# Channel attention over depthwise convolutions: edge products, transposes and mixing placed between the images of a gram, and one PSUM pool for convolution and gram

## The chip, the cores and the metric

The kernel runs on one core of a Trainium2 chip. The metric is device time in microseconds (us) of one execution, as the median of several runs. Besides, one execution was recorded by the hardware profiler; its profile and trace carry all other times here.

The engines: PE multiplies matrices (PEld is its weight load), DVE (VectorE), ACT (ScalarE) and POOL (GpSimd) work on vectors, SP issues most DMAs. PE writes PSUM alone, which has eight banks of 128 x 512 fp32 numbers. [...]

## What is computed

The input is a batch of B = 4 images with C = 192 channels of 128 x 128 pixels, fp32. Two layers follow each other. The change lies in the first, cut here to what matters:

```python
qkv = dwconv3x3(conv1x1(x, w_qkv), w_dw)      # 1x1, then a depthwise 3x3
q, k, v, l = jnp.split(qkv, 4, axis=1)
q, k, v = (heads(q), heads(k), heads(v))      # 8 heads of 24 channels: (b, 8, 24, h*w)
q = q / jnp.maximum(jnp.linalg.norm(q, axis=-1, keepdims=True), EPS)
k = k / jnp.maximum(jnp.linalg.norm(k, axis=-1, keepdims=True), EPS)
attn = jnp.einsum('bhcn,bhdn->bhcd', q, k) * temperature[None]
attn = jax.nn.softmax(attn, axis=-1)
out = jnp.einsum('bhcd,bhdn->bhcn', attn, v).reshape(b, c, h, w)
...                                            # a gate L from l
out = conv1x1(L + out + x, w_proj) + L
```

So for each head and image a 24 x 24 matrix over all 16384 pixels is needed, from q and k after their 3x3 convolution, and the norms of q's and k's channels. The second layer is a dilated local attention, and the change doesn't touch it.

## The kernel before, in words

Three stages run one after the other.

1. `project` (L382) multiplies x by the 1x1 weights, writes q and k before their 3x3 convolution to `qk_dram` in DRAM, and convolves v.
2. `channel_attention` (L671) convolves q and k, makes the attention matrices and multiplies them into the projection ("mixing", `mix1` and `mix2`), so that the second pass can apply both in one product. This is where the change lies.
3. `second_pass` (L962) applies them and does the second layer.

In stage 2, `head` (L919) is called for eight heads. A head has 48 channels to convolve: 24 of q, then 24 of k. The image's 128 rows lie on 128 partitions, in four strips of 32 rows. `loaded` (L700) fetches two channels of each of four groups for all four images, eight channels ("a source", six to a head, 2 MB each, seven DMAs on SP), into one of three buffers: two of `u` and one lent by the second pass (`lent`). It also fetches the 3x3 taps (`few`), and POOL spreads them into a band matrix (L731, L733). `convolve` (L736) multiplies one of the three columns of taps for one channel into a PSUM bank: four matmuls on four 32 x 32 parts of the array, each of which the chip runs as two weight loads and two matmuls. `order` (L925) interleaves the columns of neighbouring channels. `evicted` (L749) copies a finished bank to `conv` on ACT, and DVE takes its statistics.

A band matrix knows only its own strip. The two rows at each of the three edges between strips lack the neighbour's row there. They are made once more, by themselves, from four rows around the edge ("cut"):

- `cut_loaded` (L773) loads these rows of q and of k, 192 KB each, by two DMAs on SP. Each of the two buffers exists once, so a load waits until the product of the edge before is done with it.
- `cut_convolved` (L783) is the edge's product: six matmuls into a PSUM bank, and two copies to `s_cut` on ACT.
- `cut_turned` (L804) transposes it image by image on PE ("a turn"), and ACT copies it to `cut`.
- `cut_squares` (L812) adds its squares to the norms on DVE.

In `head` the loads for the three edges stand at channels n = 12, 28 and 44 of the order, the products after n = 14, 30 and 46, and the turns of the first two after n = 18 and 34.

`products` (L819) then makes the gram: for each of four images 32 matmuls of 128 x 96 columns accumulate in one bank (L824). After the first image stands the third turn. Then come `kept` (L831) and `part` (L837) on DVE, which pick and sum the wanted entries; the corner products of the cuts (L844, 12 matmuls); and the small sums (L854 to L862) that fold both into `logits` and give the norms. `finish` (L870) is a generator: `step` runs it one piece further after every fourth channel of the next head: norms, softmax, and in its last two pieces the mixing (L900) for two images each, its copy on DVE (L901) and its stores to `mix1` or `mix2` by DMAs on SP (L904, L907). Ahead of the heads' pieces, the same list holds those of two gates.

What sets the order: on PE the program's order is kept as written (`manual_schedule`). On the other engines and on SP's queue the framework orders instructions by the program's order among those that are ready in its own model, and sets all semaphores. PSUM is split into six banks for convolutions, edges and turns (`papc`), one for the gram and the mixing (`papg`) and one for the small sums and gates (`paps`).

Of the kernel before, what the change touches and what calls it, by code (L numbers as in the profile page):

```python
# [7 lines left out]
F32 = mybir.dt.float32  # L8
# [5 lines left out]
B, C, H, W = 4, 192, 128, 128  # L14
# [4 lines left out]
HALF = 96  # L19
# [651 lines left out]
def channel_attention(tc, d, load, qk_dram, mix1, mix2, band_p, u_p, gate_p, lent, gates):  # L671
# [7 lines left out]
    with ExitStack() as ctx:  # L679
# [4 lines left out]
        few_p = ctx.enter_context(tc.tile_pool(name="pax", bufs=2))  # L684
        st = ctx.enter_context(tc.tile_pool(name="pas", bufs=1))
        fin = ctx.enter_context(tc.tile_pool(name="paf", bufs=1))
        ps_c = ctx.enter_context(tc.tile_pool(name="papc", bufs=6, space=bass.MemoryType.PSUM))
        ps_g = ctx.enter_context(tc.tile_pool(name="papg", bufs=1, space=bass.MemoryType.PSUM))
        ps_s = ctx.enter_context(tc.tile_pool(name="paps", bufs=1, space=bass.MemoryType.PSUM))

        bands = [band_p.tile([128, 4, 2, 3, STRIP], F32, tag=f"band{k}", name=f"band{k}") for k in range(2)]
# [78 lines left out]
                both.append(t)  # L770
            return both

        def cut_loaded(hd, edge):  # L773
            us = []
            for which in range(2):
                c0 = which * C + hd * CH0
                u = cut_p.tile([4 * CH0, B * W], F32, tag=f"u{which}", name=f"cut{which}_{hd}_{edge}")
                first = (edge + 1) * STRIP - 2
                nc.sync.dma_start(u, qk_dram[first : first + 4, c0 : c0 + CH0].rearrange("r c b w -> r c (b w)"))
                us.append(u)  # L780
            return us

# [33 lines left out]
                for r in range(2):  # L816
                    nc.vector.tensor_add(sq, sq, square[:, :, which, r * CH0 : (r + 1) * CH0])

        def products(hd, q, sq, k, sk, cuts, s_cut):  # L819
            gram = ps_g.tile([HALF, B, HALF], F32, tag="gram", name=f"gram{hd}")  # L820
            for b in range(B):
                for v in range(W // 4):
                    four = lambda a: a[:, b, v].rearrange("p c w -> p (c w)")
                    nc.tensor.matmul(gram[:, b, :], four(q), four(k), start=v == 0, stop=v == W // 4 - 1)  # L824
# [12 lines left out]
            nc.vector.reduce_sum(part, kept.rearrange("p b c w -> p (b c) w"), axis=AX.X)  # L837

            two = 2 * CH0
            sums = ps_s.tile([128, SM], F32, tag="sm", name=f"sm{hd}")  # L840
            extra = sums[:two, EXTRA:].rearrange("p (b c) -> p b c", b=B)
            for b in range(B):
                for edge, cut in enumerate(cuts):
                    nc.tensor.matmul(  # L844
                        extra[:, b, :], cut[:, b, 0], cut[:, b, 1], start=edge == 0, stop=edge == 2
                    )
            own = st.tile([two, B, CH0], F32, tag="own", name=f"own{hd}")
            other = st.tile([two, B, CH0], F32, tag="other", name=f"other{hd}")
            for r, to in enumerate((own, other)):
                pick_row = same_row[:, r : r + 1].unsqueeze(1).to_broadcast([two, B, CH0])  # L850
                nc.vector.tensor_mul(to, extra[:, :, r * CH0 : (r + 1) * CH0], pick_row)
            nc.vector.tensor_add(own, own, other)
            sm = sums[:CH0]
            nc.tensor.matmul(sm[:, : B * CH0], fold, part, start=True, stop=False)  # L854
            nc.tensor.matmul(
                sm[:, : B * CH0], fold_rows, own.rearrange("p b c -> p (b c)"), start=False, stop=True
            )
            nc.tensor.matmul(
                sm[:, B * CH0 : 2 * B * CH0], ones[:, :CH0], sk.rearrange("p b c -> p (b c)"), start=True, stop=True
            )  # L860
            for b in range(B):
                nc.tensor.matmul(  # L862
                    sm[:, 2 * B * CH0 + b : 2 * B * CH0 + b + 1], sq[:, b, :], ones[:, :1], start=True, stop=True
                )
            by_image = lambda a: a.rearrange("p (b c) -> p b c", b=B)
            nc.vector.tensor_copy(logits[:, :, hd % 2, :], by_image(sm[:, : B * CH0]))
            nc.vector.tensor_copy(nk[:, :, hd % 2, :], by_image(sm[:, B * CH0 : 2 * B * CH0]))
            nc.vector.tensor_copy(nq[:, :, hd % 2], sm[:, 2 * B * CH0 : EXTRA])

        def finish(hd):  # L870


            rows, norm_q, norm_k = logits[:, :, hd % 2, :], nq[:, :, hd % 2], nk[:, :, hd % 2, :]
            wide = lambda a: a.unsqueeze(2).to_broadcast([CH0, B, CH0])
            for a in (norm_q, norm_k):
                nc.scalar.activation(a, a, AF.Sqrt)
            yield
# [12 lines left out]
            nc.vector.reciprocal(tot, tot)  # L890
            nc.vector.tensor_mul(rows, rows, wide(tot))
            yield
            yield
            low = min(max(128 - hd * CH0, 0), CH0)
            for b in range(0, B, 2):
                mixed = fin.tile([CH0, 2, C], F32, tag="mixed", name=f"mixed{hd}_{b}")
                pm = ps_g.tile([HALF, B, HALF], F32, tag="gram", name=f"pm{hd}_{b}")
                two = pm.rearrange("p b c -> p (b c)")[:CH0].rearrange("p (h o) -> p h o", h=2)
                for e in range(2):
                    nc.tensor.matmul(two[:, e, :], logits[:, b + e, hd % 2, :], wph[:, hd, :], start=True, stop=True)  # L900
                nc.vector.tensor_copy(mixed, two)  # L901
                for e in range(2):
                    if low:
                        nc.sync.dma_start(mix1[b + e][hd * CH0 : hd * CH0 + low], mixed[:low, e, :])  # L904
                    if low < CH0:
                        at = G + hd * CH0 + low - 128
                        nc.sync.dma_start(mix2[b + e][at : at + CH0 - low], mixed[low:, e, :])  # L907
                yield

        pending = [gate(ps_s) for gate in gates]  # L910

        def step():
            while pending:
# [5 lines left out]
        def head(hd):  # L919
# [6 lines left out]
            sources, pcs, sums, us, taps, s_cuts, cuts = {}, {}, [], [], [], [], []  # L926
# [22 lines left out]
            products(hd, fulls[0], sums[0], fulls[1], sums[1], cuts, s_cuts[2])  # L949
            pending.append(finish(hd))  # L950

        same, same_row, fold, fold_rows, ones, ident, wph, tempr = (
# [645 lines left out]
```

## Time and profile before

| | us |
|---|---|
| median of 3 runs | 4379.28 (4377.39 to 7416.38) |
| the profiled execution | 4374.27 |
| its span, first to last instruction | 4372.3 |
| stage 2 in the span | about 824 to 1592 |
| first convolution matmul after the small sums, heads 1 to 7 | 951.90, 1043.90, 1132.91, 1222.00, 1312.30, 1403.09, 1495.05 |
| first gram matmul, heads 0 to 7 | 926.75, 1018.74, 1107.75, 1196.84, 1287.15, 1377.93, 1469.89, 1556.11 |
| last gram matmul of the last head | 1578.3 |

The mean granted clock of PE is 0.978 of full speed. Of a line in the groups of instructions, the parts are: line, engine, operation, output and inputs, shapes, count; then busy time and mean of one in ns; then the idle time before them and what ended it. In the list of waits, "A <- B" is A's engine standing idle until B, with total us, times and the longest. "issue" is a wait whose cause the profile doesn't name. In the chain, each piece has its start and its length in us.

### The profile page before, as it was taken

The page shows a single profiled execution, that of the slowest core. Times are in us where ns is not written, and L with a number is a line of the kernel's source. Part 1 is how long each engine was busy: PE and PEld are TensorE (multiplying, and loading weights), DVE is VectorE, ACT ScalarE, POOL GpSimd, SP SyncE. Part 2 cuts the span into 40 slices and gives each one's busy share as a digit, 9 for nine tenths or more (in the row PEclk, how much of TensorE's full clock was granted, in tenths as well). Part 3 has the DMA queues.
Part 4 walks back from the last instruction along what each step waited for, and adds up shares of the span by engine and source line. Part 5 has one row for each costly group of instructions (what it writes and reads, how often), then busy time and mean ns, then how long its engine had stood idle before and what let it go on. Part 6 is the DMA issues. An engine that isn't in the chain of part 4 may idle for free.

```text
span 4372.3 us, 74543 instructions
## 1 busy us (share of the span) xinstructions
PE 4159.7 (95%) x25728; PEld 1669.8 (38%) x25728; DVE 3818.5 (87%) x5572; ACT 2632.4 (60%) x4906; POOL 3407.6 (78%) x3411
## 2 busy tenths in 40 slices
PE   8999999889899889899999999999999999999996
PEld 3333333355565543333333333333333333333331
DVE  6999999856556547899999999999999999999996
ACT  6999999734334447455665656656556566566531
POOL 6888888633323205899999999999999999999998
PEclk9999999899999999999999999999999999999997
DMA  7888888767766647656656666555555665555521
GB/s 234 265 270 251 271 274 267 217 150 171 169 156 156 165 114 157 118 124 131 131 129 133 124 133 134 126 125 130 128 130 124 137 134 124 131 130 129 116 52 32
DMA packets 476106, 676.89 MB, mean 155 GB/s; under 512 B 135937, under 2 KB 311501, under 8 KB 475729
## 3 DMA queue, kind: packets, MB, share of 16 engines
q1 hardware_dynamic: 437840, 505.39, 42.4%
q0 software_dynamic: 37888, 166.74, 20.6%
q8 instruction: 204, 3.34, 0.3%
q14 instruction: 174, 1.42, 0.1%
HBM read 278.18 MB, written 201.33 MB: 110 GB/s over the span
## 4 chain that ended last, share of the span: by engine, by line
PE 71%; DVE 14%; DMA 5%; issue 5%; POOL 3%; ACT 2%; SPq 1%; DVEq 0%; POOLq 0%; ACTq 0%
PE sc L1256 9%; PE ex L1378 8%; PE ph L1023 8%; PE pu L427 6%; PE pkv L1177 5%; PE pc L741 5%; DVE term L1384 4%; PE gram L824 4%; PE pkv L1180 4%; PE q L1237 4%; PE q L1234 4%; PE pu L432 3%; DVE prod L1245 3%; PE po L1400 2%; PE pu L578 2%
## 5 line engine op out<-in xcount | busy, mean ns | idle before, releaser
L1387 POOL TENSOR_TENSOR acc<-acc,term 128x512 f32<-128x512 f32 x1536 | 2037.6, 1332 | 144.6 <-DVE term L1384 58.2
L1384 DVE TENSOR_TENSOR term<-ex,vring 128x512 f32<-128x512 f32 (+2 forms) x1596 | 998.6, 662 | 57.3 <-PE ex L1378 44.4
L1245 DVE TENSOR_TENSOR prod<-q,kring 128x1536 f32<-128x1536 f32 (+1 forms) x600 | 1006.4, 1686 | 20.4 <-PE q L1234 10.8
L504 POOL TENSOR_TENSOR v_True<-v_True,side 128x512 f32<-128x512 f32 (+1 forms) x512 | 643.9, 1270 | 127.0 <-ACT side L493 97.9
L1378 PE MATMUL ex<-e_sb,spread 108*128 108x512 bf16 x1728 | 567.3, 387 | 49.9 <-DVE term L1384 32.5
L481 DVE SCALAR_TENSOR_TENSOR pa<-vboth,dwv,pa 128x1024 f32<-128x1024 f32 (+1 forms) x448 | 574.3, 1282 | 43.0 <-ACT pa L474 14.5
L1190 ACT COPY kring<-pkv 64x512 f32<-64x512 f32 x384 | 223.7, 583 | 415.6 <-PE pkv L1180 410.2
L1075 DVE SCALAR_TENSOR_TENSOR pa<-hboth,posw,pa 128x1024 f32<-128x1024 f32 (+1 forms) x320 | 408.1, 1275 | 37.5 <-ACT pa L1063 18.6
L1256 PE MATMUL sc<-prod,pick 128*32 128x512 f32 x3456 | 428.6, 598 | 1.8 <-DVE prod L1245 1.8
L752 DVE BATCH_NORM_STATS2 stats<-conv 128x6 f32<-128x128 f32 x1536 | 306.8, 279 | 114.9 <-ACT conv L750 112.2
L1378 PEld LDWEIGHTS <-spread 108*128 108x128 bf16 x1728 | 133.3, 97 | 661.3 <-issue 641.0
L1023 PE MATMUL ph<-lent,mix 128*64 128x512 f32 (+1 forms) x1024 | 375.5, 598 | 1.8 <-DMA mix<-mixed 1.8
L427 PE MATMUL pu<-xt,wx 128*128 128x512 f32 x768 | 360.6, 613 | 17.2 <-ACT vboth L463 10.2
L1403 ACT COPY o<-po 128x512 f32<-128x512 f32 x192 | 106.3, 588 | 446.2 <-PE po L1400 240.0
L1177 PE MATMUL pkv<-y,wkv 128*128 128x512 f32 x768 | 363.7, 595 | 9.5 <-DMA y<-moved 9.3
L493 ACT ACTIVATE side<-ring,dwv 128x512 f32<-128x512 f32 (+1 forms) x512 | 348.4, 725 | 31.8 <-POOL v_True L504 27.9
L733 POOL COPY band<-few 32x6 f32<-32x6 f32 x384 | 75.3, 199 | 372.0 <-PE pc L741 247.6
L1107 ACT ACTIVATE side<-hring,posw 128x512 f32<-128x512 f32 (+1 forms) x512 | 341.7, 713 | 11.7 <-DMA side<-side 9.8
L750 ACT COPY conv<-pc 128x512 f32<-128x512 f32 x384 | 216.8, 586 | 187.4 <-PE pc L741 178.4
L741 PE MATMUL pc<-u,band 32*32 32x508 f32 (+1 forms) x6144 | 281.3, 624 | 36.6 <-issue 22.1
L1190 ACT COPY vring<-pkv 64x512 f32<-64x512 f32 x384 | 224.3, 584 | 45.5 <-PE pkv L1180 32.6
L427 PEld LDWEIGHTS pu<-xt,wx 128*128 128x128 f32 x768 | 143.1, 193 | 225.6 <-issue 122.3
(170 smaller groups left out, 6514.2 us busy)
## 6 DMA issues: line engine op xcount, KB each, us to landing
qk_dram<-us SPq DMA_DIRECT2D x192, 512.0 KB
side<-side POOLq DMA_DIRECT2D x124, 768.0 KB, 7.3
xt<-in_x SPq DMA_DIRECT2D x64, 512.0 KB
v_dram<-v_False SPq DMA_DIRECT2D x64, 512.0 KB
lent<-in_x SPq DMA_DIRECT2D x128, 256.0 KB
lent<-v_dram SPq DMA_DIRECT2D x128, 256.0 KB
y<-moved POOLq DMA_DIRECT2D x64, 512.0 KB, 5.2
out<-o SPq DMA_DIRECT2D x128, 256.0 KB
```

The costliest lines, as they stand in the source:

```text
L427: mm(pu, wx[:, mt * 128 : (mt + 1) * 128], tiles["xt", n][:, im, :], start=True, stop=False)
L481: nc.vector.scalar_tensor_tensor(by_row(to[:, o : o + length]), by_row(vboth[:, at : at + length, :, t % 3 : t % 3 + W]), dwv[:, 0, t : t ...
L504: nc.gpsimd.tensor_add(v[:, rows, :], v[:, rows, :], z[:, rows, :])
L741: nc.tensor.matmul(pc[r * STRIP : (r + 1) * STRIP, :, to], band[at, e, c, dx, :], u[at, e, c, :].rearrange("p (b w) -> p b w", w=W)[:, :, of],
L1023: mm(to, w[:, cols], tiles["xv", n, j, im], start=j == 0, stop=j == 2)
L1177: mm(rows3(tile_of("pc", key)), w, tiles["y", n, im], start=True, stop=False)
L1190: nc.scalar.copy(rows[HALVES[im], :, pad : pad + W], rows3(tiles["pkv", n, pair, im])[HALVES[e]])
L1245: nc.vector.tensor_mul(to[:, :, px].rearrange("p t (r w) -> p t r w", w=W), q.unsqueeze(1).to_broadcast([128, 3, *q.shape[1:]]), three,)
L1256: mm(sc[quad * 32 : (quad + 1) * 32, :], pick[:, QR - 4 * row : QR - 4 * row + 32], tiles["prod", n, k // NT, k % NT // 3][:, k % 3, :], s ...
L1378: mm(rows3(tile_of("ex", ("ex", n, g, t))), spread[:, t, :], e_sb, start=True, stop=True)
L1384: nc.vector.tensor_mul(rows3(to[:, px]), rows3(ex[:, px]), win)
L1387: nc.gpsimd.tensor_add(tiles["acc", n, g], tiles["acc", n, g], tiles.pop(("term", n, g, t)))
```

## The change

It touches stage 2 alone.

- The pool of the gram goes. Convolutions, edges, turns and now the gram share one pool of seven banks. The mixing takes its bank from the pool of the small sums.
- The load of the first edge stands at n = 24 on SP. The loads of the second and third edge are issued by ACT, each directly after the product of the edge before.
- The three edge products stand in `products`, each ahead of one of the first three images of the gram; each turn and its squares stand after that image.
- The mixing becomes a generator of its own (`mix`), which the last piece of `finish` puts into a list. Its two halves run in the middle of the first and of the second image of the next head's gram, and its stores are issued by ACT. The last head's mixing runs behind the last head.
- The corner products stand in the middle of the fourth image, and their sums on DVE ahead of `kept`. The products for the norms come before the two that fold `part` and the corner sums.

```diff
-        ps_c = ctx.enter_context(tc.tile_pool(name="papc", bufs=6, space=bass.MemoryType.PSUM))
-        ps_g = ctx.enter_context(tc.tile_pool(name="papg", bufs=1, space=bass.MemoryType.PSUM))
+        ps_c = ctx.enter_context(tc.tile_pool(name="papc", bufs=7, space=bass.MemoryType.PSUM))
...
-        def cut_loaded(hd, edge):
+        def cut_loaded(hd, edge, queue):
...
-                nc.sync.dma_start(u, qk_dram[first : first + 4, c0 : c0 + CH0].rearrange("r c b w -> r c (b w)"))
+                queue.dma_start(u, qk_dram[first : first + 4, c0 : c0 + CH0].rearrange("r c b w -> r c (b w)"))
...
-        def products(hd, q, sq, k, sk, cuts, s_cut):
-            gram = ps_g.tile([HALF, B, HALF], F32, tag="gram", name=f"gram{hd}")
+        def products(hd, q, sq, k, sk, us, taps):
+            gram = ps_c.tile([128, B, W], F32, tag="pc", name=f"gram{hd}")[:HALF, :, :HALF]
+            cuts, two = [], 2 * CH0
             for b in range(B):
+                if b < 3:
+                    s_cut = cut_convolved(hd, b, us, taps)
+                    if b < 2:
+                        us = cut_loaded(hd, b + 1, nc.scalar)
                 for v in range(W // 4):
+                    if v == W // 8 and b < 2 and mixes:
+                        next(mixes[0], None)
+                        if b:
+                            mixes.pop()
+                    if (b, v) == (3, W // 8):
+                        sums = ps_s.tile([128, SM], F32, tag="sm", name=f"sm{hd}")
+                        extra = sums[:two, EXTRA:].rearrange("p (b c) -> p b c", b=B)
+                        for im in range(B):
+                            for edge, cut in enumerate(cuts):
+                                nc.tensor.matmul(
+                                    extra[:, im, :], cut[:, im, 0], cut[:, im, 1], start=edge == 0, stop=edge == 2
+                                )
                     four = lambda a: a[:, b, v].rearrange("p c w -> p (c w)")
                     nc.tensor.matmul(gram[:, b, :], four(q), four(k), start=v == 0, stop=v == W // 4 - 1)
-                if b == 0:
-                    cuts.append(cut_turned(hd, 2, s_cut))
-                    for edge, cut in enumerate(cuts):
-                        cut_squares(hd, edge, cut, (sq, sk))
+                if b < 3:
+                    cuts.append(cut_turned(hd, b, s_cut))
+                    cut_squares(hd, b, cuts[b], (sq, sk))
...
-            yield
-            yield
+            mixes.append(mix(hd))
+
+        def mix(hd):
+
             low = min(max(128 - hd * CH0, 0), CH0)
             for b in range(0, B, 2):
                 mixed = fin.tile([CH0, 2, C], F32, tag="mixed", name=f"mixed{hd}_{b}")
-                pm = ps_g.tile([HALF, B, HALF], F32, tag="gram", name=f"pm{hd}_{b}")
-                two = pm.rearrange("p b c -> p (b c)")[:CH0].rearrange("p (h o) -> p h o", h=2)
+                pm = ps_s.tile([128, SM], F32, tag="sm", name=f"pm{hd}_{b}")
+                two = pm[:CH0, : 2 * C].rearrange("p (h o) -> p h o", h=2)
...
-                        nc.sync.dma_start(mix1[b + e][hd * CH0 : hd * CH0 + low], mixed[:low, e, :])
+                        nc.scalar.dma_start(mix1[b + e][hd * CH0 : hd * CH0 + low], mixed[:low, e, :])
...
-                    if n in (12, 28, 44):
-                        edge = len(us)
-                        taps = taps or cut_taps(hd)
-                        us.append(cut_loaded(hd, edge))
+                    if n == 24:
+                        taps = cut_taps(hd)
+                        us = cut_loaded(hd, 0, nc.sync)
...
-                if n in (14, 30, 46):
-                    s_cuts.append(cut_convolved(hd, len(s_cuts), us[len(s_cuts)], taps))
-                if n in (18, 34):
-                    cuts.append(cut_turned(hd, len(cuts), s_cuts[len(cuts)]))
...
+            for left in mixes:
+                for _ in left:
+                    pass
```

More of the change, by code (lines that the diff above doesn't have):

```diff
@@ L830, in products @@
+            own = st.tile([two, B, CH0], F32, tag="own", name=f"own{hd}")
+            other = st.tile([two, B, CH0], F32, tag="other", name=f"other{hd}")
+            for r, to in enumerate((own, other)):
+                pick_row = same_row[:, r : r + 1].unsqueeze(1).to_broadcast([two, B, CH0])
+                nc.vector.tensor_mul(to, extra[:, :, r * CH0 : (r + 1) * CH0], pick_row)
+            nc.vector.tensor_add(own, own, other)
             kept = st.tile([128, B, CH0, 4], F32, tag="square", name=f"kept{hd}")[:HALF]
@@ L837, in products @@
             nc.vector.reduce_sum(part, kept.rearrange("p b c w -> p (b c) w"), axis=AX.X)
[L839 to L852, printed above, removed]
             sm = sums[:CH0]
[L854 to L857, printed above, removed]
             nc.tensor.matmul(
@@ L864, in products @@
                 )
+            nc.tensor.matmul(sm[:, : B * CH0], fold, part, start=True, stop=False)
+            nc.tensor.matmul(
+                sm[:, : B * CH0], fold_rows, own.rearrange("p b c -> p (b c)"), start=False, stop=True
+            )
             by_image = lambda a: a.rearrange("p (b c) -> p b c", b=B)
@@ L903, in finish @@
                     if low:
-                        nc.sync.dma_start(mix1[b + e][hd * CH0 : hd * CH0 + low], mixed[:low, e, :])
+                        nc.scalar.dma_start(mix1[b + e][hd * CH0 : hd * CH0 + low], mixed[:low, e, :])
                     if low < CH0:
                         at = G + hd * CH0 + low - 128
-                        nc.sync.dma_start(mix2[b + e][at : at + CH0 - low], mixed[low:, e, :])
+                        nc.scalar.dma_start(mix2[b + e][at : at + CH0 - low], mixed[low:, e, :])
                 yield
-        pending = [gate(ps_s) for gate in gates]
+        pending, mixes = [gate(ps_s) for gate in gates], []
         def step():
@@ L925, in head @@
             order = sorted((0.75 * n + k, n, dx) for n in range(2 * CH0) for k, dx in enumerate((1, 0, 2)))
-            sources, pcs, sums, us, taps, s_cuts, cuts = {}, {}, [], [], [], [], []
+            sources, pcs, sums = {}, {}, []
             for _, n, dx in order:
@@ L942, in head @@
                     step()
-                if n in (14, 30, 46):
-                    s_cuts.append(cut_convolved(hd, len(s_cuts), us[len(s_cuts)], taps))
-                if n in (18, 34):
-                    cuts.append(cut_turned(hd, len(cuts), s_cuts[len(cuts)]))
                 if n % CH0 == CH0 - 1:
                     sums.append(squares(hd, which, stats[which]))
-            products(hd, fulls[0], sums[0], fulls[1], sums[1], cuts, s_cuts[2])
+            products(hd, fulls[0], sums[0], fulls[1], sums[1], us, taps)
             pending.append(finish(hd))
```

## The prediction

> **What bounds the kernel now.** I read the page first, then busy times by stretch, the waits, the chain and the timeline of the attention stage, then the records of packets and semaphores behind the DMA view.
>
> ```profile
> PE 4159.7 (95%) x25728; PEld 1669.8 (38%) x25728; DVE 3818.5 (87%) x5572; ACT 2632.4 (60%) x4906; POOL 3407.6 (78%) x3411
> ...
> L741 PE MATMUL pc<-u,band 32*32 32x508 f32 (+1 forms) x6144 | 281.3, 624 | 36.6 <-issue 22.1
> ```
>
> The change lies in one stage, from about 824 to 1592 us. Busy times of one head there (columns: stretch, length, then PE, PEld, DVE, ACT, POOL, granted clock, DMA share, GB/s):
>
> ```profile
> 1107.00:1196.00 89.00, 81.28 (x1502) 53.51 (x1502) 52.08 (x239) 34.90 (x63) 28.11 (x72) 0.96 0.68 162
> ```
>
> PE bounds a head: DVE has 52 us of 89 and ACT 35. So what PE waits for is what counts (the waits of the stage; total us, times, longest):
>
> ```profile
> PEld pc L741 <- issue: 126.7, 199, 5.4
> ...
> PE pc L741 <- issue: 37.2, 22, 4.1
> PEld pcut L789 <- DMA cut<-qk_dram: 16.1, 7, 4.1
> ...
> PE pcut L789 <- DMA cut<-qk_dram: 13.0, 8, 3.6
> ...
> PE gram L824 <- ACT conv L750: 7.6, 8, 1.0
> ```
>
> The timeline of PE shows the kinds one by one:
>
> ```profile
> 1057.36 2.77 PE L789 MATMUL pcut<-cut,cuttaps 96*48 96x512 f32 x12
> ...
> 1072.56 3.84 PE L741 MATMUL pc<-lent,band 32*32 32x508 f32 x104 [2.18 <-issue]
> ...
> 1101.37 4.46 PE L789 MATMUL pcut<-cut,cuttaps 96*48 96x512 f32 x10 [3.16 <-DMA cut<-qk_dram]
> 1105.76 1.05 PE L741 MATMUL pc<-u,band 32*32 32x508 f32 x8
> 1107.76 5.68 PE L824 MATMUL gram<-conv,conv 128*96 128x96 f32 x64 [0.94 <-ACT conv L750]
> ```
>
> A strip-edge product takes 2.77 us, but ten twelfths of one take 4.46 after a wait of 3.16. The "issue" stops are code arriving: counted over PE's queue, those over 0.5 us lie whole multiples of 256 instructions apart, and PE goes on 1.3 to 1.7 us after the end of a 16 KB packet of this queue (one per 256 instructions):
>
> ```profile
> q8 instruction: 96, 1.57, 0.9%
> ...
> cut<-qk_dram SPq DMA_DIRECT2D x48, 192.0 KB
> ```
>
> With idle DMA a block of 256 convolution instructions takes 4.0 to 4.3 us; between 1040 and 1556, the 22 blocks whose packet saw no cut transfer under way average 4.77 us, the 17 that did 7.01 us.
>
> The chain shows the cut transfers (start, us):
>
> ```profile
> 1089.64 11.69 DMA cut<-qk_dram
> 1101.37 4.47 PE pcut L789 x7
> ...
> 1107.76 5.68 PE gram L824 x64
> 1113.87 16.32 PE gram L824 x192
> 1130.19 1.22 PE sm L844 x24
> ...
> 1543.60 7.78 DMA cut<-qk_dram
> ```
>
> These durations run from the issue of a pair's second transfer to its landing. From the first issue, the 24 pairs take 8.6 to 15.4 us: 8.6 to 9.5 with nothing queued ahead, 10.2 to 11.2 in the steady heads' gram, 13.1 to 15.4 behind u loads. A cut transfer's semaphore takes one step at once and four later; a u transfer's takes sixteen. So four engines carry each pair, one transfer after the other.
>
> **The change, part by part.** From the starts of convolution, heads 1 to 6 take (1495.05 - 951.90) / 6 = 90.5 us each: 65.3 convolution with products, turns and mixing in it, and 25.2 gram and after.
>
> *Convolution without products.* It has 2304 weight loads and matmuls and some 26 semaphore waits: 9.1 blocks. The cut transfers for edges 1 and 2 leave this stretch. Nearest row: the 4.77 us blocks, so 43.4 us; the u loads now keep DMA busy for nearly all of it, and the no-cut blocks under such load took 5.05 to 5.92, so at most 1.5 x 4.2 + 7.6 x 5.6 = 49. I take 47. SP loses four cut loads and four stores a head (0.66 to 0.84 us each to issue), and the stores no longer hold u loads behind them (two at 1253.73, the rest at 1259.17). PE waited for u 0.9 us at most at a time in a steady head, so that is worth 0 to -1, and I take 0: three u buffers cover it, and without them the u loads are what is late next. POOL's queue keeps its work.
>
> *Gram stretch.* Gram 5.68 + 16.32 = 22.0; three products x 2.70 (chain) = 8.1; three turns x 0.59 = 1.8; eight mixing matmul records x 0.16 = 1.3; the 24 corner products 1.2. After the gram: kept 0.55 and part 0.55 on DVE (were beside the corner products' 1.22) then fold and fold_rows, 0.3 each, about 1.9 in all. Sum 36.3. The 0.94 wait for the last eviction goes, since the first product stands before the gram.
>
> *The new waits.* One cut buffer per side: the transfers for edge b+1 start when product b ends and product b+1 needs both. Between them PE has one image of gram (5.5), mixing (0.65) and a turn (0.55): 6.7 us. ACT issues them; no ACT issue is in the trace, so 0 to 0.84 us each by SP's issues, and they stand behind two copies of 0.58 in program order, so the first goes 0 to 1.3 us after the product. Landing from there 8.6 to 15.4. Edge 1: wait from 8.6 - 6.7 = 1.9 to 1.3 + 15.4 - 6.7 = 10.0. The next head's last u load starts when convolution ends and runs about 9 us (2.1 MB at the 240 GB/s seen from 1229 to 1238), so it is nearer the loaded rows; they queued behind u loads on one queue and a second queue need not, so 12 rather than 14: 1.2 + 12 - 6.7 = 6.5. Edge 2: little else moves then, 1.2 + 8.8 - 6.7 = 3.3, up to 10.0. After such waits the clock falls (granted 0.51 from 1256 to 1259 after a 1.83 us wait): ten records took 4.46 instead of 2.3 after 3.16, 5.25 after 3.57 + 2.39 with two records between. So 0 to 3 each, I take 4.5 for both. Together 14.3 per head, between 4 and 26. Behind the ACT issues stand only copies of turns and s_cut, on which no later product but the turn itself waits; the mixing's stores wait for DVE's copy (0.54) and are issued before the turn. Edge 0 is loaded in the previous gram, with 47 us to land: 0.
>
> *Head:* 47 + 36.3 + 14.3 = 97.6 against 90.5: +7.1, six times +43. Head 7 (61.1 + 25.2 before; no next loads): 45 + 36.3 + 2 x 3.3 + 2 x 2.2 = 92.3, +6. Head 0 waits for POOL's bands during convolution (chain: 4 x 0.78 at 875), so the two moved products were partly covered: gram stretch 35 + 15.6 against 25.2, less 2.75 for the third product, 0.9 for the eviction and half of the other two and their turns, 3.3: +18.5. Evictions get a seventh bank: PE's waits for them in steady heads outside the gram row are under 1 us, so 0. DVE's squares and corner sums move beside gram, where DVE waited 115.6 us for it: 0. The last head's mixing stays behind it: 0. Sum +67.
>
> [...]
>
> [...]
>
> **Rivals.**
> 1. *The forecast*, edge loads late by 3 to 8 us: 4400 to 4475.
> 2. *Not slower:* the edge loads are issued at once, share engines well and land at 8.6 to 9. Waits 1.9 to 2.3 each and little lost clock, 5 per head; convolution 43.4. Head 84.7, six times -5.8, head 7 -4, head 0 about +8: -31, some 4348. It decides where the waits and lost clock fall under 90.5 - 47 - 36.3 = 7.2 us per head. For it: the no-cut blocks. Against it: no pair in 24 landed within 8.6 us.
> 3. *Slower by over 2%:* both rings full on four engines. Waits 10 and 7, clock 6, convolution 49: head 108, six times +18, heads 0 and 7 +40: +147, some 4526. For it: pairs at 15.3 us. Against: edge 2 meets an emptier DMA.
> 4. *Convolution isn't relieved,* as the products no longer give code time to arrive: blocks of 5.75 (mean of all 39), 52 us: 8 x 5 = 40 more than the forecast, some 4486. Against it: the split 4.77 to 7.01.
>
> **How the numbers follow.** The profiled execution took 4374.27 us (span 4372.3); the median shown is 4379.28, 5 above it. 4374 + 67 = 4441, and with the median's 5 us: 4446. Chances: forecast 0.56, not slower 0.20, both-rings 0.12, unrelieved 0.12. The range 4375 to 4505 leaves out most of rival 2's lower half and the end of rival 3, about 0.2; the forecast's own is 4400 to 4475. Two per cent is 88 us, about what a measurement of this kernel can tell from no change, so 4467 is the bound: rivals 3 and 4 lie over it (0.22, less 0.02) and a sixth of the forecast (0.10): slower 0.30. Faster needs 4292, below every case: 0.02. Same 0.68.
>
> **What would show it.** Right: pcut waiting for "DMA cut" at the second and third product of each head, 3 us or more, and slow records behind; gram stretch near 50 us; convolution near 47 with fewer long "issue" stops; no 0.94 before gram. Wrong: those waits near 2 or absent (rival 2), or convolution above 52 (rival 4).

## The result, and the profile after

The changed kernel takes 4425.59 us (median of 4417.64 to 4430.37) against 4378.34 for the kernel before, measured beside it. The ratio is 1.0112, with a 95% interval of 1.0089 to 1.0135: slower by 1.1%, within the 2% of the prediction's middle class and 20 us below its number. (The 7416.38 among the runs before is left out of every ratio.) The profiled execution has a span of 4415.9 us against 4372.3: 43.6 more.

Where it lies, by the starts of convolution: head 0 ends 8.4 us later (960.31 against 951.90), heads 1 to 6 take 96.7 us each instead of 90.5 (37.2 in all), head 7 takes as long as before (86.7 and 86.6 to the last small sums). The second pass gives 2 us back. One steady head by stretch (columns as in the prediction):

```profile
1154.99:1251.37 96.38, 81.98 (x1503) 54.01 (x1502) 52.81 (x239) 34.97 (x62) 27.81 (x72) 0.95 0.61 153
```

PE's work has hardly grown (82.0 us busy in this head; in the prediction's window of the kernel before, 81.3 in 89); its idle time has. The waits of the stage (total us, times, longest):

```profile
PEld pc L740 <- issue: 168.9, 186, 26.2
PE pc L740 <- issue: 64.3, 33, 4.3
...
PE pcut L788 <- DMA cut<-qk_dram: 30.7, 13, 5.9
...
PEld pcut L788 <- DMA cut<-qk_dram: 17.5, 7, 3.2
...
PE sm L867 <- DVE part L858: 5.4, 7, 0.8
```

"issue" ahead of the convolution went up from 37.2 to 64.3, though less work stands in it; the products' wait for their loads went up from 13.0 to 30.7; gram's wait for the last eviction (7.6) is gone. PE's timeline shows where the products wait:

```profile
1109.49 2.77 PE L788 MATMUL pcut<-cut,cuttaps 96*48 96x512 f32 x12
...
1122.94 1.14 PE L788 MATMUL pcut<-cut,cuttaps 96*48 96x512 f32 x2 [3.71 <-DMA cut<-qk_dram]
1125.35 5.33 PE L788 MATMUL pcut<-cut,cuttaps 96*48 96x512 f32 x10 [1.28 <-DMA cut<-qk_dram]
...
1137.58 2.77 PE L788 MATMUL pcut<-cut,cuttaps 96*48 96x512 f32 x12
...
1154.44 0.34 PE L867 MATMUL sm<-part,fold 96*24 96x96 f32 x2 [0.78 <-DVE part L858]
```

The first product of a head meets its data. The second waits, and its ten records then take 5.33 us instead of 2.3. The third doesn't wait at all. The same head in the chain (start, length, what):

```profile
1075.40 2.63 issue
1078.03 6.10 PE pc L740 x121
...
1089.62 2.81 issue
1092.44 5.97 PE pc L740 x125
1098.40 2.52 issue
1100.92 8.64 PE pc L740 x224
...
1113.21 12.10 DMA cut<-qk_dram
...
1125.35 5.33 PE pcut L788 x8
```

So there are two costs: 9 us of "issue" in a convolution of 52.7, and one late pair of transfers (q's and k's load for one edge). In the trace after, the 25 stops over 0.5 us ahead of a convolution matmul in heads 1 to 6 lie whole multiples of 256 of PE's instructions apart (to within two), and each ends 1.3 to 1.7 us after the end of a 16 KB packet of the instruction queue; that queue has 95 such packets from 820 to 1640 us, for some 24,400 instructions of PE, so one for a block of 256 (about 128 matmuls and as many weight loads). The stops thus fall where PE has reached the next block before its code has arrived, which is called late code below.

To compare kernels, PE's matmul records of heads 1 to 6 were laid on one line: each share of time goes to the kind of record that covers it, each gap to the record behind it. A gap counts as late code where the record behind it starts 1.1 to 1.9 us after the end of a 16 KB packet of code. Records are called slow where their pace is about half the usual one, as in the ten that took 5.33 us: the clock granted from 1125 to 1128 us was 0.50. In inconv, mix_moved, hybrid, hybrid_sp and mixconv, 0.3 to 1.3 us of the late code are gaps before a product, a turn or a small sum, nearly all of which the profile puts to another wait that ended at about the same time. The runs in the table are told in the next section. Per head, in us:

| kernel | head | convolution | late code | products | their wait for loads | other waits | gram | mixing | turns, sums |
|---|---|---|---|---|---|---|---|---|---|
| before | 90.5 | 45.0 | 5.5 | 10.3 | 2.0 | 1.6 | 22.0 | 0.1 | 3.9 |
| after | 96.7 | 43.5 | 9.3 | 11.3 | 3.8 | 0.8 | 22.9 | 1.5 | 3.6 |
| early | 90.5 | 44.1 | 9.2 | 8.1 | 0.0 | 1.1 | 22.8 | 1.5 | 3.7 |
| inconv | 94.5 | 43.5 | 4.1 | 12.1 | 4.7 | 1.7 | 22.9 | 1.5 | 3.9 |
| mix_moved | 94.9 | 44.2 | 5.0 | 12.1 | 3.8 | 1.4 | 23.0 | 1.5 | 3.9 |
| hybrid | 91.4 | 44.1 | 3.5 | 8.1 | 0.0 | 6.2 | 23.6 | 1.5 | 4.3 |
| hybrid_sp | 92.7 | 44.1 | 4.3 | 8.3 | 0.0 | 7.0 | 23.0 | 1.5 | 4.4 |
| mixconv | 92.0 | 45.2 | 3.8 | 8.6 | 0.0 | 7.2 | 22.7 | 0.1 | 4.3 |
| pooled | 93.9 | 47.2 | 9.6 | 9.2 | 0.0 | 1.6 | 22.2 | 0.1 | 3.9 |
| rows | 99.0 | 44.3 | 9.7 | 11.6 | 4.5 | 0.8 | 23.1 | 1.5 | 3.6 |
| no_u_before | 76.7 | 41.1 | 0.0 | 8.1 | 0.0 | 1.5 | 22.0 | 0.1 | 3.9 |
| no_u | 75.3 | 38.0 | 0.0 | 8.6 | 0.0 | 0.8 | 22.8 | 1.5 | 3.6 |
| early_mix | 89.5 | 44.2 | 8.8 | 8.9 | 0.1 | 1.4 | 22.4 | 0.1 | 3.7 |
| halves | 87.4 | 43.7 | 2.7 | 9.6 | 0.0 | 4.5 | 22.8 | 0.0 | 4.0 |

### The profile page after: what moved, and what is told of

It reads as the page before. It is cut to its first block, busy times and chain, and to the rows that moved or that the text cites. A ratio compares the mean times of both kernels' runs of the same rounds, so it can differ in the third digit from the quotient of the medians.

```text
span 4415.9 us, 74471 instructions
## 1 busy us (share of the span) xinstructions
PE 4162.3 (94%) x25728; PEld 1689.4 (38%) x25728; DVE 3819.6 (86%) x5572; ACT 2629.8 (60%) x4906; POOL 3402.4 (77%) x3411
## 4 chain that ended last, share of the span: by engine, by line
PE 69%; DVE 14%; issue 6%; POOL 5%; DMA 4%; ACT 2%; SPq 0%; ACTq 0%; POOLq 0%; DVEq 0%
PE sc L1262 8%; PE pc L740 8%; PE ex L1384 8%; PE ph L1029 7%; PE pu L427 6%; PE pkv L1183 5%; DVE term L1390 4%; PE pkv L1186 4%; PE q L1243 3%; PE q L1240 3%; PE gram L840 3%; PE pu L432 3%; POOL acc L1393 3%; DVE prod L1251 3%; PE pu L578 2%
## 5 line engine op out<-in xcount | busy, mean ns | idle before, releaser
L1251 DVE TENSOR_TENSOR prod<-q,kring 128x1536 f32<-128x1536 f32 (+1 forms) x600 | 1005.1, 1684 | 21.5 <-PE q L1240 11.0
L427 PE MATMUL pu<-xt,wx 128*128 128x512 f32 x768 | 358.4, 610 | 18.5 <-ACT vboth L463 11.0
```

Of the source, the lines that this page charges most:

```text
L427: mm(pu, wx[:, mt * 128 : (mt + 1) * 128], tiles["xt", n][:, im, :], start=True, stop=False)
L1251: nc.vector.tensor_mul(to[:, :, px].rearrange("p t (r w) -> p t r w", w=W), q.unsqueeze(1).to_broadcast([128, 3, *q.shape[1:]]), three,)
```

## The experiments

Theory: the late pair, and code that arrives late in a convolution that has nothing else in it. Rivals: the pair alone; the shared PSUM pool, the mixing or the new order behind the gram.

**early.** A second set of cut buffers, so that every edge load goes out a product or more ahead; the corner sums lie in the statistics' tile, which is dead by then, to make room.

```diff
-                u = cut_p.tile([4 * CH0, B * W], F32, tag=f"u{which}", ...)
+                u = cut_p.tile([4 * CH0, B * W], F32, tag=f"u{which}_{(hd + edge) % 2}", ...)
...
-                    if b < 2:
-                        us = cut_loaded(hd, b + 1, nc.scalar)
+                    of, edge = (hd, 2) if b == 0 else (hd + 1, b - 1)
+                    if of < HEADS0:
+                        ahead[of, edge] = cut_loaded(of, edge, nc.scalar)
```

> The change, with a second set of cut buffers, so that every edge load goes out in the gram stretch a whole product or more ahead (edge 2 of this head after its first product, edges 0 and 1 of the next head after the second and third). Theory (two costs: the second product's late load with its slow records, some 4.8 us per head; and code that arrives late in a convolution that has no other work in it, 8.9 us of issue stops per head where there were 5.4): no product waits for a DMA, heads 1 to 6 take 92 us instead of 96.7, convolution stays at 52 to 53, the time falls by 30 to 35 to about 4392. Rival A (the edge waits alone made the change slower): down by 45 or more, 4380 or less. Rival B (the convolution is the bound whatever stands before it, and takes back what the waits give): 4415 or more.

4380.62 us, ratio to the kernel before 1.0018 (1.0007 to 1.0028), so 0.9% below the change, some 41 us. No product waits, and none is slow (11.3 to 8.1): 7.0 us per head together, of which 6.2 reach the head. It lies between the theory and rival A: the slow records were worth 3.2, not the 1 that the expectation's 4.8 had left for them. But the other half of the theory stands, as the convolution's stops are unchanged:

```profile
PE pc L740 <- issue: 65.3, 32, 4.0
```

So without the late pair 0.9 of the 1.1% are gone. That the convolution was relieved of its products gave nothing in the end: late code took 9.2 us per head there, 5.5 in the kernel before.

**inconv.** The edges back at their old places, the rest of the change kept.

```diff
+                if n in (14, 30, 46):
+                    s_cuts.append(cut_convolved(hd, len(s_cuts), us[len(s_cuts)], taps))
+                if n in (18, 34):
+                    cuts.append(cut_turned(hd, len(cuts), s_cuts[len(cuts)]))
```

> The change with the edge loads, the edge products and their transposes back at their old places in the convolution; seven banks, gram in one of them, mixing between the images, its stores on ACT's queue, the corner products in gram and the late fold stay. Theory (all that costs time is in where the edges stand): convolution with its products near 64 us, issue stops of the convolution back near 5.5 us per head, within 0.3 per cent of the kernel before, 4365 to 4392. Rival C (the shared PSUM pool, the mixing in gram or the later fold cost time): 4405 or more.

4402.16 us, 1.0069 (1.0053 to 1.0084). The theory fell here: with the edges back, six tenths of the loss stayed. Late code does fall, from 9.3 to 4.1, but the products wait 4.7 us and are slow. Rival C is as good as met (4405), so its parts were taken singly.

**mix_moved.** The kernel before, with the mixing alone between gram's images.

```diff
-            yield
-            yield
+            mixes.append(mix(hd))
...
+                    if v == W // 8 and b < 2 and mixes:
+                        next(mixes[0], None)
...
-                        nc.sync.dma_start(mix1[b + e][hd * CH0 : hd * CH0 + low], mixed[:low, e, :])
+                        nc.scalar.dma_start(mix1[b + e][hd * CH0 : hd * CH0 + low], mixed[:low, e, :])
```

> The kernel before with one part of the change alone: the mixing between the first two images of gram, in the bank of the small sums, stores on ACT's queue. Theory: 1.4 us per head that the convolution hid, 8 to 12 more than before (ratio 1.002 to 1.003), edge waits as before (2 us per head). Rival F (the mixing gave the edge loads time, and without it they come late, as in the run with the edges back in the convolution: 4.7 us of waits per head): 20 to 32 more. Rival G (the longer waits and the 32 us there come from the seven banks): 0 to 5 more, or faster, as the stores no longer stand in SP's queue.

4394.19 us, 1.0053 (1.0035 to 1.0072): 23 us, rival F. The banks are thus not needed to explain inconv. The mixing costs 1.5 us on PE's path instead of 0.1, gram's pieces 1.0 more, and the third product comes too soon for its pair (1.8 us more of waits per head, and 1.8 more in the products, which run slow behind them):

```profile
1096.10 1.90 PE L789 MATMUL pcut<-cut,cuttaps 96*48 96x512 f32 x2 [4.66 <-DMA cut<-qk_dram]
1099.62 5.33 PE L789 MATMUL pcut<-cut,cuttaps 96*48 96x512 f32 x10 [1.62 <-DMA cut<-qk_dram]
```

There the pair goes out at 1084.2, and PE wants it 7.2 us later; in the kernel before it went out at 1087.9, and PE came to the product 9.3 us later. Both the shorter way of PE and the stores that no longer hold u loads in SP's queue can be behind it; the runs don't separate them. The 0.5% here and the 0.9% of the late pair in early aren't parts of one sum: most of what the moved mixing costs here is again a late pair.

**no_u and no_u_before.** The u loads of heads 1 to 7 are left out of the change and of the kernel before, by the same edit.

```diff
-            if turn % 3 == 0:
+            if hd:
+                u = lasting[turn % 3]
+            elif turn % 3 == 0:
...
-            for e in range(4):
+            lasting[turn % 3] = u
+            for e in range(0 if hd else 4):
```

> The change without the u loads of heads 1 to 7: their convolutions read the three tiles that head 0 left, so 12.6 MB per head are not moved and the output is that of other data. Theory (code held back by the u loads): issue stops under 2 us per head, convolution 38 to 42 us instead of 53, edge pairs land in 6.5 to 7 us from their first issue and the second product waits 1 us or less, a head takes 78 to 83 us. Rival (the convolution is bound by PE, by evictions into the seven banks or by POOL's bands): convolution 48 or more.

> The kernel before without the u loads of heads 1 to 7, left out in the same way as in the run of the change without them (the output is that of other data). What the change costs where no u load disturbs it. Theory (apart from the u loads the change only exposes the mixing, 1.4 us per head, and cuts gram into more pieces, 0.8, and saves gram's wait of 0.9): 73.5 to 74.5 us per head against 75.3 there; all other idle time gone. Rival (the change does relieve PE, and only the u loads hid it): 76 or more.

Single runs took 4269.37 and 4274.87 us. In both traces, in heads 1 to 6, every stop for code, every wait for an edge load and nearly every slow record is gone, with as many instructions and as much code (columns as above):

```profile
1030.00:1400.00 370.00, 366.90 (x7434) 290.73 (x7421) 250.89 (x1186) 173.88 (x308) 140.52 (x360) 1.00 0.10 29
```

```profile
1030.00:1400.00 370.00, 363.10 (x7264) 254.75 (x7243) 257.03 (x1166) 170.58 (x302) 142.15 (x359) 1.00 0.10 29
```

The first line is of the change, the second of the kernel before. PE is busy 99% and 98%, at a granted clock of 1.00. The convolution of the change then takes 38.0 us, 15 less than with the u loads: what holds code back are the u transfers. The records of packets show how: a packet of code starts 0.8 us (median) after PE enters a block without the u loads, and 3.2 us after it in the change; those that PE waited for there started 2.4 to 6.3 us after. And the second expectation's rival was right: without u loads the change is faster, 75.3 against 76.7 us per head in one profile of each (75.1 to 75.7 and 76.7 to 76.8 in the six heads). From the starts of the eighth matmul ahead and behind, less the usual pace, a product among convolution matmuls lengthens PE's way by 3.3 us instead of 2.77 and a turn by 0.85 instead of 0.44 to 0.6, and gram's wait of 0.98 goes; against that stand 1.5 for the mixing, which costs 0.01 us a matmul among the convolution's 32 x 32 tiles, and 0.8 for gram in pieces. So the u transfers turn a gain of 1.4 us per head into a loss of 6.2: they cost the kernel before 13.8 us per head (90.5 - 76.7) and the change 21.5.

**rows.** Each edge load cut into one transfer for each image row.

```diff
-                queue.dma_start(u, qk_dram[first : first + 4, c0 : c0 + CH0].rearrange("r c b w -> r c (b w)"))
+                for r in range(4):
+                    queue.dma_start(
+                        u[r * CH0 : (r + 1) * CH0],
+                        qk_dram[first + r, c0 : c0 + CH0].rearrange("c b w -> c (b w)"),
+                    )
```

> The change with each edge load cut into four, one for each image row, so that the slowest dimension of the source is 24 channels instead of 4 rows. Theory (a pair is slow because four engines carry it): a row's transfer lands in 2 to 3 us instead of 4.4 to 12, its semaphore goes up in one step, the last of eight lands about 8 us after the first issue (eight issues of 0.7 on ACT and one landing), the second product waits 1 to 2 us instead of 3.8 and few slow records follow: 15 to 30 below the change. Rival (a ring shared with the u loads, or the issue itself, sets the landing): as the change or slower, 4410 or more.

4429.41 us, 1.0133 (1.0112 to 1.0155): no gain. The part on the engines holds as far as the records go: a row's transfer (24 channels) raises its semaphore in twelve late steps (the expectation had one) and lands 1.6 to 1.9 us after its issue where little else moves. In the change, a transfer of four rows raises it in four late steps and lands in 4.4 to 6.1 us with no u transfer under way, and while edge loads are under way four 2 KB packets run at a time for 58% of the time, more for 11%. That four engines carry it is read from this; the records don't name a packet's engine. But ACT couldn't issue the eight in a row: after four issues within 4 us the fifth came 5 us later (922.88, 923.22, then 928.15), and the products waited 4.5 us instead of 3.8. In the trace after, the 1992 DMAs of SP and ACT share eight semaphores, 249 on each, and none is issued before the last step of the transfer that had its semaphore before; 117 come within 0.1 us of that step, the nearest 0.016 us behind it. So it is here: the issue at 928.15 came 0.02 us after the last step of the u transfer that SP had issued at 917.67.

**hybrid, hybrid_sp, mixconv, pooled.** Products in the convolution, loads ahead in two sets. They differ in who issues the loads. The diff is hybrid's: in hybrid_sp and mixconv the first of the two loads stands at n = 40 on `nc.sync`, in pooled both are on `nc.gpsimd`. In mixconv and pooled the mixing stands in the convolution again, with its stores on POOL.

```diff
+                    s_cuts.append(cut_convolved(hd, len(s_cuts), ahead.pop((hd, len(s_cuts))), taps))
+                    if n == 14:
+                        ahead[hd, 2] = cut_loaded(hd, 2, nc.scalar)
...
+                    if hd + 1 < HEADS0:
+                        for edge in range(2):
+                            ahead[hd + 1, edge] = cut_loaded(hd + 1, edge, nc.scalar)
```

> As the run with the edges back in the convolution, but with two sets of cut buffers: edges 0 and 1 of a head are loaded in the gram of the head before, only edge 2's pair is under way during convolution, with half a convolution to land. Theory: no product waits for a DMA any more (2.5 us per head of waits and some slow records), and the u loads, not the cut loads, are what holds code back, so 4350 to 4372, 10 to 25 below the kernel before. Rival D (as the prediction's split of the blocks into 4.77 and 7.01 us had it: cut transfers under way hold code back): two of three pairs less in convolution are worth 4 us per head more, 4325 to 4345. Rival E (the products' waits are hidden by other waits): the same as before, 4375 or more.

> As the run with two sets of cut buffers and the products in the convolution, with edge 2's pair issued by SP behind the u load of block 5 instead of by ACT behind the first product. Theory (there ACT's issue stood waiting for a u load up to 10.3 us, with its copies behind it, so the first transpose waited 3.35 us per head, with 0.9 of late code, and gram 2.1 instead of 0.9): these go, 4.5 to 5 us per head, 30 to 35 in all: 4335 to 4355, below the kernel before by 0.4 to 0.8 per cent. Rival (the edge loads among the u loads hold code back as much as ACT's wait cost): 4365 or more.

> The run above with the mixing back among the convolution's matmuls, at the steps where the kernel before has it, its stores issued by POOL. Theory (the mixing's 24x24 matmuls take one 32x32 tile and run beside the convolution's: in the kernel before they lengthened PE's path by 0.14 us per head, between the gram's images by 1.5): 1.3 us per head, 8 to 12 below the run above. Rival (the copies or the stores get in the way of evictions or bands, or one more thing in the convolution delays the products): equal to the run above or slower.

> Products and mixing in the convolution, two sets of cut buffers, as in the run with the mixing back there, but every edge load ahead is issued by POOL, whose transfers take no turns with the u loads' semaphores. Theory (ACT stood at an edge load's issue until a u load landed, 9.8 us at a time with s_cut behind it, and the second transpose and gram waited for that): the transposes' 4.6 us of waits per head, 0.7 of late code with them and 0.8 at gram go: 5 to 6 us per head, 35 to 42 below that run, 4335 to 4350, 0.5 to 0.8 per cent below the kernel before. Rival (the code stops only move: what PE does not wait for the transposes it waits for code): 4365 or more.

4378.0 (1.0016, 1.0007 to 1.0025), 4385.33 (1.0031, 1.0021 to 1.0041), 4380.2 (1.0018, 1.0006 to 1.0030) and 4401.1 (1.0053, 1.0036 to 1.0071). All four theories missed. In hybrid, hybrid_sp and pooled the time lies where the rival had it (4375, 4365 and 4365 or more). Hybrid's product waits went, 24 us below inconv, but it isn't below the kernel before, so neither the theory's gain nor rival D's came: other waits, 6.2 us per head, for a turn and for gram, took their place, as rival E had it. Hybrid_sp moved one pair to SP, and the framework pulled the next head's loads on ACT ahead of `s_cut` instead (ACT's timeline of hybrid_sp):

```profile
1093.37 0.69 ACTq L778 DMA_DIRECT2D cut<-qk_dram  x1
1094.16 1.17 ACT L800 COPY s_cut<-pcut 48x512 f32<-48x512 f32 x2 [9.81 <-DMA u<-qk_dram]
```

ACT stands 9.8 us for a u transfer, and the turn behind it makes PE wait 5.6. Pooled takes ACT out of it; those waits go (7.2 to 1.6), and the late code comes in their place (3.8 to 9.6), as its rival had it:

```profile
PE pc L740 <- issue: 56.8, 22, 5.4
```

That fits a simple reading: where PE stood anyway, code had time to arrive, and where it doesn't stand, it waits for code. It is argued, not shown: pooled's edge loads also go by POOL's own queue, and no run tells what that does to the code. Mixconv against hybrid_sp doesn't decide on the mixing, as the intervals overlap.

**early_mix.** Early, with the mixing among the convolution's matmuls and its stores on POOL.

```diff
-            mixes.append(mix(hd))
+            yield
+            yield
+            yield from mix(hd)
...
-                        nc.scalar.dma_start(mix1[b + e][hd * CH0 : hd * CH0 + low], mixed[:low, e, :])
+                        nc.gpsimd.dma_start(mix1[b + e][hd * CH0 : hd * CH0 + low], mixed[:low, e, :])
```

> The change with its edge loads ahead in two sets of buffers, as before, and the mixing back among the convolution's matmuls, its stores issued by POOL. Theory: the mixing is hidden again, 1.4 us per head less in gram, and the convolution's PE time does not grow: 8 to 12 below the run with the mixing in gram, 4368 to 4376, level with the kernel before. Rival (a stretch with the mixing in it stops as often for code, and the copies delay evictions): as that run or slower.

4362.85 us, 0.9982 (0.9967 to 0.9997): below the kernel before, by a little. Per head 1.0 us less than early: the mixing's 1.5 are hidden, 0.8 come back in products.

**halves.** Early_mix, each u transfer cut into two.

```diff
+                    half = (to.stop - to.start) // 2
+                    for at in (0, half):
...
-                        u[to, e].rearrange("p c w -> p (c w)"),
-                        qk_dram[of, first : first + 2].rearrange("h c b w -> h (c b w)"),
+                            u[to.start + at : to.start + at + half, e].rearrange("p c w -> p (c w)"),
+                            qk_dram[of.start + at : of.start + at + half, first : first + 2].rearrange(
...
```

> The run with edge loads ahead and the mixing in the convolution, with every u transfer cut into two of half the rows, so that with the same eight semaphores in turn at most half as many bytes stand in the rings. Theory (a packet of code stands behind the u bytes already queued, 2.5 to 5.4 us): the packets start 1 to 3 us sooner, the convolution's late code falls from 8.6 us per head to 5 to 6, 15 to 25 below that run, 4335 to 4350. Rival (the packet shares a busy memory, however much is queued, or SP's fourteen issues of 0.4 us make the u loads late): code stops stay at 8 or more, 4360 or more.

4340.75 us, 0.9929 (0.9916 to 0.9943): the fastest, 0.7% below the kernel before and by the ratios 0.5% below early_mix, with the same bytes and the same work on PE. The waits between 951 and 1500 us in early_mix, then in halves:

```profile
PE pc L740 <- issue: 49.2, 24, 4.0
```

```profile
PE turned L810 <- ACT s_cut L804: 21.1, 6, 5.2
PE pc L744 <- issue: 18.0, 20, 2.4
```

Late code falls from 8.8 to 2.7 us per head, more than expected, and the longest stop from 4.0 to 2.4. Of the 6 us, 3.5 come back as waits for a turn: ACT again stands at a load's issue until a u transfer lands (62.9 us in nine waits ahead of its copies to `s_cut`, 11.5 at the longest). A packet of code now starts 2.1 us (median) after PE enters a block, against 2.8 in early_mix. That fewer bytes stand ahead of a code packet is what the edit was to do; that it is this and not another effect of more and smaller transfers is argued, not shown.

The heads of the table are not the whole gain. The profiled execution is 36.6 us shorter than early_mix's: 12.6 in heads 1 to 6, 5.0 in head 7, 15.7 in head 0 and 3.3 outside these heads. In head 0 early_mix has a wait that halves hasn't:

```profile
908.94 10.93 PE L740 MATMUL pc<-u,band 32*32 32x512 f32 x216 [10.52 <-POOL band L730]
```

The taps that POOL spreads into bands, issued at 885.96 in early_mix, landed 9.3 us later; those issued at 882.29 in halves landed after 5.1. In these two profiles a good part of the gain thus comes from taps that landed sooner, not from less late code.

## Why the prediction was right, and where it wasn't

The number was right for partly wrong reasons, and so partly by luck: the convolution came out 5.6 us longer than its term and the two waits for loads 6.0 us shorter than theirs, and these two misses cancelled. By the prediction's own sign (convolution above 52) it was rival 4 that had the convolution right.

1. *Convolution without products, 47: 52.6 measured (43.5 and the 9.1 of late code that stand in it).* This step failed. It went by the split of blocks: 4.77 us without a cut transfer under way, 7.01 with one, and took the cut transfers for the cause. In the profile after, no cut transfer is under way in any block of convolution between 1055 and 1600, and the 49 blocks average 5.8. The u transfers hold code back, and the cut transfers only stood beside them: in no_u_before the cut transfers still run during the convolution, and not one stop for code is left in heads 1 to 6. So rival 4, with its chance of 0.12, was right on the convolution (52 us, and late code halved where the products stand in the convolution again, inconv); its sum of 4486 wasn't met, as it kept the forecast's waits. Late code is 9.3 us per head in the change with the u transfers and 0.0 without them.
2. *Gram stretch without new waits, 36.3: 37.1* (44.1 less the waits and slow records below). Right; gram in pieces is 0.8 dearer, which was left out.
3. *Edge 1, 6.5: 3.8.* The mechanism and the landing were right: the pairs of heads 1 to 6 take 9.5 to 14.4 us from first issue, 12.1 on average, for the 12 taken. ACT issued them within 0.1 us of the product, where 1.2 had been added, and two of twelve matmuls start on the first transfer.
4. *Edge 2, 3.3: 0.0.* The landing was mis-sized: 6.5 to 7.0 us, below all 24 pairs before. Those that had nothing queued ahead (8.6 to 9.5) had u transfers (in head 7's last pair, loads of the second pass) issued right behind them; the new ones have none. The queue isn't the reason: edge 0's pairs, which SP issues in the change with no u load behind them, take 6.4 to 6.8, and SP's pairs in no_u_before take 6.8 to 7.8 in heads 1 to 7. The prediction read "nothing queued ahead" where "nothing behind either" was needed.
5. *Lost clock, 4.5: 3.2* (products 11.3 instead of 8.1, all behind edge 1's wait).
6. *Per head 97.6: 96.7.* Head 0 was put at +18.5 and cost 8.4. Of the 10 us between, 5.4 lie in its convolution, where PE's wait for POOL's bands fell from 13.2 to 5.3 us, so that more than the half taken was covered, and 4.7 in its gram stretch (45.9 against 35 + 15.6). Head 7 was put at +6 and cost nothing: its pairs meet no u load, and no product waits.
7. *SP's freed queue, 0; seven banks, 0; the 0.94 before gram, gone:* as predicted, the banks as far as inconv (1.0053 to 1.0084) and mix_moved (1.0035 to 1.0072) can't be told apart. The mixing was booked at 1.3 in gram (1.5 measured); that nearly all of it is new cost wasn't said: among the convolution's matmuls the mixing had cost 0.01 us a matmul, 0.1 us a head.

Rivals 2 and 3 didn't come: the first needed a convolution of 43.4, the second a wait at edge 2.

## What to carry to other kernels

A stall that falls on blocks beside transfer A isn't A's if B is always there as well: look for blocks with B alone, or take B away in a run. Where PE stops for code beside big transfers, work that is moved out of the stretch may only leave more time to wait for code (5.5 us a head became 9.3 here). Load what is needed before the stretch (the products' wait for loads went from 3.8 us a head to 0.0 in early), leave small matmuls where they cost nothing (0.1 us a head here against 1.5), and try the big transfers in halves (late code went from 8.8 us a head to 2.7 here). And an issue placed on a computing engine can hold that engine until someone else's transfer has landed (ACT for 9.8 us in hybrid_sp).

## What the runs showed of the hardware

- The u transfers, not PE's work, set 13.8 of 90.5 us per head in the kernel before, though in heads 1 to 6 PE waits 0.9 us at most at a time for u itself: 5.5 as late code, 2.0 as waits for edge loads, and some 6 as longer time of PE's records (convolution 45.0 against 41.1, products 10.3 against 8.1), at a granted clock of 0.97 over heads 1 to 6 against 1.00 without them.
- Halving each u transfer took 6 us of late code from a head with the bytes unchanged, of which 2.1 us reached the head's time.
- A 192 KB edge load in four rows lands in 4.4 to 6.1 us with no u transfer under way, and in up to 13.6 with u transfers (both in the change); a quarter of it over 24 channels in 1.6 to 1.9 where little else moves (rows).
